# An order-only edge that places GpSimd's normalising product behind an addition of exponentials

## The chip, the cores and the metric

The kernel runs on one core of one Trainium2 chip. The metric is the device time of one execution in microseconds (us), as the median of several runs. For the kernel before it is 4073.38 us (three runs, 4070.07 to 4077.61).

## What is computed

Two layers on x of shape (2, 256, 64, 64), all in float32. The first is attention with 8 heads of depth 32 over n = 4096 positions, the second a non-local block with one softmax over 1024 pooled keys. Nearly all the time goes into the first, and the change lies in it:

```python
qkv = jnp.einsum('oc,bchw->bohw', w_qkv, x)
q, k, v = jnp.split(qkv, 3, axis=1)          # each reshaped to (b, 8, 32, 4096)
scores = jnp.einsum('bhdi,bhdj->bhij', q, k) / jnp.sqrt(jnp.asarray(d, x.dtype))
attn = jax.nn.softmax(scores, axis=-1)
out = jnp.einsum('bhij,bhdj->bhdi', attn, v)
return jnp.einsum('oc,bchw->bohw', w_proj, out.reshape(b, c, h, w)) + x
```

The softmax is normalised late: the kernel sums exp(scores - max) times v (the numerator, `num`) and exp(scores - max) alone (the denominator, `den`), and multiplies `num` by 1/`den` at the end of a block.

## The kernel before

**Tiling.** A block is one batch entry b, one group of four heads (`qd`, 0 or 1) and 512 queries (`i`, 0 to 7). There are 2 x 2 x 8 = 32 blocks, numbered 0 to 31 here in their order of time; n = 2b + qd is the index of the group of four heads, so blocks 0 to 7 have n = 0 and blocks 24 to 31 have n = 3. After blocks 15 and 31 come the output projection (`project`) and the second layer (`non_local`) of one batch entry.

**One block.** `attend` loops over j = 0 to 31, 128 keys at a time. In step j, for two pairs of heads, TensorE makes the scores into PSUM (line 401, with line 413 putting the maximum in first), and ScalarE takes the exponential (line 537): 128 x 1024 values for heads 0 and 1 into a tile of its own (`single`), and as many for heads 2 and 3 into one half of a double tile `two` (`double`), which serves j and j + 1. One step later TensorE multiplies by v (line 425, eight matmul pieces in the profile, into `w`), and VectorE adds `w` to `num` (line 436). Between these, TensorE, VectorE and ScalarE work on the maxima of a later block (lines 252, 264, 271, 278), cut into single steps by a generator. At some odd steps, q, k or v of a later block are made as well: in a block with i < 6, k and v of the next group at j = 15 and a q at j = 27. For n = 3 there is no next group, so these blocks have no k and v work at j = 15.

**The denominator** is summed on two roads. GpSimd adds the tile for heads 0 and 1 into the block's first such tile (line 455, called `added`). The double tiles of heads 2 and 3 are summed by DMAs that add while they write (line 463): GpSimd issues one for each pair of steps, into two running sums by turns. Each DMA holds its double tile until it has landed. There are `TWOS = 5` double tiles: two are the running sums, three go round, so the exponential of pair P writes to the tile that pair P - 3 has given back.

**Normalising** (`normalize`) of a block runs as a generator inside the next block: at j = 2 GpSimd issues a DMA that joins the two running sums (line 469); at j = 6 TensorE sums over partitions (`den`, line 481) and ScalarE copies the result to `r` (line 489); at j = 7 two DMAs on the SP queue spread the few distinct values over partitions (lines 498, 499); at j = 12 VectorE takes the reciprocals (line 503), and five DMAs on SP write them back and broadcast them into `r` (lines 504, 506); after 13 more steps, at j = 25, comes the product of line 511 on GpSimd, `y = num * r`. `advance(normal)` stands behind `add(blk, j, p, two)` in the loop, so at this point `added` is the addition of step j = 25 of the running block (of j = 24 in block 31, where VectorE takes the odd steps from GpSimd).

**Order.** The order in which instructions stand in an engine's queue isn't that of the source: a scheduler in the compiler chooses it by its own estimates of when operands are ready, and each engine then works through its queue in that order. `tc.issue_after(ins)` adds an edge without a semaphore: what is traced inside the block stands behind `ins` in the queue. The kernel has such edges already, for the joining DMA (line 468), the reciprocals (line 502) and the exponentials (line 536). In the built program of the kernel before, the product of line 511 stands directly behind the addition of step j = 13 in 29 of the blocks (j = 8 in block 31), and ahead of the DMA of line 463 for j = 12 and 13 (j = 8 and 9).

The pools that matter:

```python
    ONES, TWOS = 6, 5
    def single(name):
        return probs.tile([P, 2, NB], F32, tag="one", name=name, bufs=ONES)
    def double(name):
        return probs.tile([P, 2, 2, NB], F32, tag="two", name=name, bufs=TWOS)
```

Of the kernel before, what the change touches and what calls it, by code (L numbers as in the profile page):

```python
# [24 lines left out]
NB = 512  # L25
# [10 lines left out]
def conv_attention(  # L36
# [13 lines left out]
    nc = tc.nc  # L50
# [20 lines left out]
    def scratch(name):  # L71
        return ps_m.tile([P, NB], F32, tag="m", name=name)
# [303 lines left out]
    def attend(b, y):  # L376
# [65 lines left out]
        added = None  # L442
# [22 lines left out]
        def normalize(blk):  # L465
            whole = [1, 2]
            if (blk.qd, blk.i) != (QUADS - 1, NI - 1):
                with tc.issue_after(added.ins):
                    nc.gpsimd.dma_start(out=blk.sums[1], in_=blk.sums[2], accum_op=ALU.add)
                whole = [1]  # L470
                yield
            den = scratch(f"den_{blk.name}")
            mine = [
                [blk.sums[0], *blk.last],
                [blk.sums[n][:, j] for j in range(2) for n in whole],
            ]
            for n in range(max(map(len, mine))):
                for h in range(QH):
                    those = mine[h // 2]
                    if n < len(those):  # L480
                        nc.tensor.matmul(  # L481
                            den[bass.ts(h, D), :],
                            ones[:, :D],
                            those[n][:, h % 2, :],
                            start=(n == 0),
                            stop=(n == len(those) - 1),
                        )
            r = work.tile([P, NB], F32, tag="r", name=f"r_{blk.name}", bufs=1)
            nc.scalar.copy(r, den)
            yield  # L490
            if (blk.qd, blk.i) == (QUADS - 1, NI - 1):
                nc.vector.reciprocal(r, r)
            else:


                flat = [spare.tile([QH, NB], F32, tag=f"flat{a}", name=f"flat{a}_{blk.name}") for a in range(2)]
                few = work.tile([P, NB // D], F32, tag="few", name=f"few_{blk.name}")
                nc.sync.dma_start(out=flat[0], in_=r[::D, :])
                nc.sync.dma_start(out=few, in_=flat[0].rearrange("h (c e) -> (h c) e", c=D))
                for _ in range(5):  # L500
                    yield
                with tc.issue_after(reduced.ins):
                    nc.vector.reciprocal(few, few)
                nc.sync.dma_start(out=flat[1].rearrange("h (c e) -> (h c) e", c=D), in_=few)
                for h in range(QH):
                    nc.sync.dma_start(
                        out=r[bass.ts(h, D), :], in_=flat[1][h : h + 1, :].broadcast_to([D, NB])
                    )
                for _ in range(13):
                    yield  # L510
            nc.gpsimd.tensor_mul(y[:, blk.qd, bass.ts(blk.i, NB)], blk.num, r)

        waiting, normal = None, iter(())
        for qd in range(QUADS):
            for i in range(NI):
                blk = Block(qd, i)
# [3 lines left out]
                for j in range(NJ):  # L520
# [17 lines left out]
                    if waiting is not None:  # L538
                        weigh(*waiting)
                        if j == 0:  # L540
                            normal = normalize(waiting[0])
# [8 lines left out]
                    elif items and j in ((15, 27), (11, 19, 27))[len(groups) - 2]:  # L550
                        for item in items.pop(0):
                            advance(make(*item), 9)
        weigh(*waiting)
        return normalize(blk)


# [225 lines left out]
    for b in range(B):  # L782
        y = big.tile([P, NC, N], F32, tag="y", name=f"y{b}")
# [56 lines left out]
```

## Time and profile before

| what | value |
|---|---|
| median of 3 runs | 4073.38 us |
| the profiled execution: its time, its span in the trace | 4072.18 us, 4070.4 us |
| PE busy | 4021.6 us, 99% |
| DVE busy | 2974.8 us, 73% |
| ACT busy | 2673.8 us, 66% |
| POOL busy | 2892.5 us, 71% |
| granted TensorE clock, mean | 0.996 |
| line 511, the product: count, mean | 32, 1270 ns |
| POOL idle ahead of line 511 | 207.6 us |
| line 463, the adding DMA: count, median from issue to landing | 448, 7.6 us |

PE is TensorE, DVE VectorE, ACT ScalarE, POOL GpSimd, SP the engine that issues most plain DMAs. In the lists of waits, a row says who waited for whom, the total in us, how often, and the longest. In a timeline, a row has the start in us, the length in us, engine, line, operation, tiles and count; a bracket gives the idle time of the engine just before, and what ended it. A busy PE isn't a PE at its peak, since matmuls are pipelined and overlap in the records.

### The profile page before, as it was taken

What the parts mean: (1) busy time and instruction counts of PE and PEld (TensorE: products, weight loads), DVE (VectorE), ACT (ScalarE), POOL (GpSimd) and SP (SyncE); (2) the same over time, 40 slices, a digit from 0 to 9 for tenths busy, and PEclk for the clock granted to TensorE, in tenths of its full rate; (3) what the DMA queues carried; (4) which work ended last, traced back from release to release, by engine and by line L of the source; (5) the groups of instructions that cost most, each with busy time, mean ns of one, the idle gap of its engine ahead of it and who ended that gap; (6) DMA issues with size and microseconds to landing.
All of it is one profiled execution on the core that took longest, in us unless ns stands there. A gap on an engine that the chain in (4) does not pass through costs nothing.

```text
span 4070.4 us, 75211 instructions
## 1 busy us (share of the span) xinstructions
PE 4021.6 (99%) x29616; PEld 1495.2 (37%) x29616; DVE 2974.8 (73%) x5451; ACT 2673.8 (66%) x3329; POOL 2892.5 (71%) x1844
## 2 busy tenths in 40 slices
PE   9999999999999999999999999999999999999998
PEld 4333333333333333333333333333333333332333
DVE  5877877788778777774457777777888888784444
ACT  5777777777777777751147777777677777776111
POOL 0888887778778888761457888787888888776143
PEclk9999999999999999999999999999999999999999
DMA  1677777777777777780027777778777777778200
GB/s 59 143 161 161 155 164 160 159 162 164 156 161 163 165 161 160 165 197 0 25 51 159 161 161 162 165 160 173 161 165 161 158 155 164 154 151 173 76 16 26
DMA packets 113380, 569.35 MB, mean 140 GB/s; under 512 B 20232, under 2 KB 22024, under 8 KB 51840
## 3 DMA queue, kind: packets, MB, share of 16 engines
q0 software_dynamic: 68832, 501.25, 60.5%
q1 hardware_dynamic: 42928, 62.10, 5.0%
q8 instruction: 232, 3.80, 0.4%
q10 hardware_dynamic: 1264, 1.19, 0.1%
q14 instruction: 124, 1.02, 0.1%
HBM read 54.39 MB, written 8.88 MB: 16 GB/s over the span
## 4 chain that ended last, share of the span: by engine, by line
PE 89%; DMA 5%; DVE 2%; POOL 1%; issue 1%; ACT 1%; SPq 0%; POOLq 0%; DVEq 0%; ACTq 0%
PE ps L252 27%; PE w L425 23%; PE s L401 17%; PE y L698 5%; PE s L413 5%; DMA p<-p 3%; DMA flat<-few 2%; PE q L195 2%; PE den L481 1%; PE k L195 1%; PE proj L567 1%; PE g L623 1%; PE v L183 1%; DVE r L712 1%; PE f L666 1%
## 5 line engine op out<-in xcount | busy, mean ns | idle before, releaser
L455 POOL TENSOR_TENSOR p<-p,p 128x1024 f32<-128x1024 f32 x945 | 2331.0, 2467 | 444.5 <-ACT p L537 308.1
L252 PE MATMUL ps<-k,q 32*128 32x512 f32 x6232 | 2116.6, 618 | 2.4 <-DVE part L278 1.0
L537 ACT ACTIVATE p<-s 128x1024 f32<-128x1024 f32 x2048 | 1987.3, 1026 | 134.2 <-PE ps L252 46.1
L264 DVE TENSOR_REDUCE part<-ps 128x1 f32<-128x512 f32 x2136 | 1372.6, 686 | 138.2 <-PE s L401 66.4
L425 PE MATMUL w<-p,v 128*32 128x512 f32 x8192 | 1093.4, 605 | 0.0
L278 DVE CUSTOM_DVE_ANT_0 ps<-ps,over 128x512 f32<-128x512 f32 x980 | 683.8, 700 | 540.3 <-PE ps L252 299.1
L401 PE MATMUL s<-q,k 32*128 32x512 f32 x4096 | 1038.0, 594 | 0.0
L271 ACT ACTIVATE over<-ps 128x512 f32<-128x512 f32 x916 | 546.9, 597 | 578.2 <-PE ps L252 533.9
L252 PEld LDWEIGHTS ps<-k,q 32*128 32x128 f32 x6232 | 788.8, 184 | 261.6 <-DVE num L436 75.4
L436 DVE TENSOR_TENSOR num<-num,w 128x512 f32<-128x512 f32 x992 | 671.7, 677 | 42.3 <-PE w L425 39.4
L252 PE MATMUL ps<-kd,q 32*128 32x512 f32 x1056 | 568.4, 643 | 1.0 <-POOL kd L214 0.7
L401 PE MATMUL s<-q,last_kd 32*128 32x512 f32 x2048 | 515.2, 616 | 12.1 <-ACT p L537 12.1
L401 PE MATMUL s<-q,kd 32*128 32x512 f32 x2048 | 513.1, 617 | 2.0 <-ACT p L537 2.0
L252 PE MATMUL ps<-last_kd,q 32*128 32x512 f32 x904 | 482.1, 640 | 1.5 <-POOL last_kd L214 1.5
L425 PEld LDWEIGHTS w<-p,v 128*32 128x32 f32 x8192 | 161.5, 108 | 778.9 <-ACT over L271 689.4
L463 POOL DMA_DIRECT2D p<-p x448 | 388.4, 867 | 70.7 <-ACT p L537 67.4
L413 PE MATMUL s<-rows,ones_b 32*128 32x512 bf16 x2048 | 394.5, 381 | 0.1
L401 PEld LDWEIGHTS s<-q,k 32*128 32x128 f32 x4096 | 371.3, 184 | 10.6 <-issue 7.2
L413 PEld LDWEIGHTS <-ones_b 32*128 32x128 bf16 x2048 | 132.6, 91 | 504.4 <-PE ps L252 251.6
L401 PEld LDWEIGHTS s<-q,last_kd 32*128 32x128 f32 x2048 | 172.5, 184 | 232.4 <-ACT p L537 219.9
L401 PEld LDWEIGHTS s<-q,kd 32*128 32x128 f32 x2048 | 174.8, 185 | 224.4 <-ACT p L537 196.8
L698 PE MATMUL y<-p,kv 128*128 128x512 f32 x512 | 240.0, 608 | 6.4 <-DVE r L712 6.4
(106 smaller groups left out, 2239.7 us busy)
## 6 DMA issues: line engine op xcount, KB each, us to landing
p<-p POOLq DMA_DIRECT2D x478, 1024.0 KB, 7.6
x_k<-in_x_dram SPq DMA_DIRECT2D x32, 512.0 KB
x_q<-in_x_dram SPq DMA_DIRECT2D x30, 512.0 KB
x_res<-in_x_dram SPq DMA_DIRECT2D x16, 512.0 KB
out_dram<-z SPq DMA_DIRECT2D x16, 512.0 KB
r<-flat SPq DMA_DIRECT2D x120, 64.0 KB
x_v<-in_x_dram SPq DMA_DIRECT2D x6, 512.0 KB
wqk_sb<-in_wqk_dram ACTq DMA_DIRECT2D x1, 512.0 KB
```

What stands on the lines that cost most here:

```text
L252: nc.tensor.matmul(ps, q[n, i][bass.ts(h, D), bass.ts(g, P)], keys[bass.ts(h, D), :], start=True, stop=True,)
L264: reduced = nc.vector.tensor_reduce(part[:, g, h, j : j + 1], ps, AX.X, ALU.max)
L271: cut = nc.scalar.activation(over, ps, AF.Relu)
L278: reduced = nc.vector.tensor_tensor_reduce(out=ps, in0=ps, in1=over, scale=1.0, scalar=LEAST, op0=ALU.add, op1=ALU.max, accum_out=part[:, ...
L401: nc.tensor.matmul(s[:, t, :], kj[bass.ts(h, D), :], q[blk.n, blk.i][bass.ts(h, D), :], start=False, stop=True, skip_group_check=j % 2 == 1,)
L413: nc.tensor.matmul(s[:, t, :], ones_b[bass.ts(h, D), :], rows[blk.rows][bass.ts(h, D), :], start=True, stop=False,)
L425: nc.tensor.matmul(w[bass.ts(h, D), :], v[blk.n][:, keys(j), h, :], p[h // 2][:, h % 2, :], start=True, stop=True,)
L436: nc.vector.tensor_add(blk.num, blk.num, w)
L455: added = nc.gpsimd.tensor_add(blk.sums[0], blk.sums[0], p[0])
L463: nc.gpsimd.dma_start(out=blk.sums[n], in_=two, accum_op=ALU.add)
L537: nc.scalar.activation(p[pair], s, AF.Exp, scale=scale)
L698: nc.tensor.matmul(acc[i][o], wg[:, 2 * t + j, bass.ts(o, P)], p[:, j, :], **edge)
```

## The change

The product of line 511 is put inside an `issue_after` block, so that it can't stand ahead of the last addition of exponentials that was traced before it:

```diff
                 for _ in range(13):
                     yield
-            nc.gpsimd.tensor_mul(y[:, blk.qd, bass.ts(blk.i, NB)], blk.num, r)
+            with tc.issue_after(added.ins):
+                nc.gpsimd.tensor_mul(y[:, blk.qd, bass.ts(blk.i, NB)], blk.num, r)
```

In the built program 30 of the 32 products move. In 29 blocks the product goes from behind the addition of j = 13 to behind that of j = 25, and stands ahead of the DMA of line 463 for j = 24 and 25; in block 31 it goes from behind j = 8 to behind j = 24. The two products that belong to blocks 15 and 31 themselves, which are made in `project`, stay where they were. The queues of TensorE, VectorE, ScalarE and SP hold the same instructions in the same order as before, and the product waits for the same semaphores (four DMAs and VectorE).

## The prediction

> **What bounds the kernel now.** I read the page first: the busy times, then the chain that ended last.
>
> ```profile
> span 4070.4 us, 75211 instructions
> PE 4021.6 (99%) x29616; PEld 1495.2 (37%) x29616; DVE 2974.8 (73%) x5451; ACT 2673.8 (66%) x3329; POOL 2892.5 (71%) x1844
> PE 89%; DMA 5%; DVE 2%; POOL 1%; issue 1%; ACT 1%; SPq 0%; POOLq 0%; DVEq 0%; ACTq 0%
> ```
>
> TensorE is busy all the time, so an idle GpSimd costs nothing by itself. But 5% of the chain is DMA, which a kernel bound by TensorE alone wouldn't have. So I read the list of waits for the product and for what GpSimd feeds.
>
> ```profile
> POOL y L511 <- DMA r<-flat: 138.5, 25, 8.0
> POOL y L511 <- DVE r L492: 42.7, 2, 21.6
> POOL y L511 <- DVE part L264: 20.3, 4, 6.8
> ACT p L537 <- DMA p<-p: 25.9, 21, 3.2
> ```
>
> The product waits at the head of GpSimd's queue for the broadcast of reciprocals. Of 207.6 us, 42.7 belong to the two products in the projection, which stay; 164.9 us over 30 products are 5.5 us each. The last row matters: exponentials wait for adding DMAs. The timelines of block 29 (GpSimd, ScalarE, TensorE) show how one leads to the other.
>
> ```profile
> 3515.95 2.36 POOL L455 TENSOR_TENSOR p<-p,p 128x1024 f32<-128x1024 f32 x1 [0.57 <-ACT p L537]
> 3525.14 1.28 POOL L511 TENSOR_TENSOR y<-num,r 128x512 f32<-128x512 f32 x1 [6.83 <-DVE part L264]
> 3526.36 0.87 POOL L463 DMA_DIRECT2D p<-p  x1
> 3526.97 5.11 POOL L455 TENSOR_TENSOR p<-p,p 128x1024 f32<-128x1024 f32 x2
> ```
> ```profile
> 3534.29 1.02 ACT L537 ACTIVATE p<-s 128x1024 f32<-128x1024 f32 x1 [3.18 <-DMA p<-p]
> ```
> ```profile
> 3532.12 0.59 PE L252 MATMUL ps<-k,q 32*128 32x512 f32 x1
> ...
> 3535.37 0.70 PE L401 MATMUL s<-q,last_kd 32*128 32x512 f32 x2 [2.66 <-ACT p L537]
> ```
>
> The addition of j = 13 ends at 3518.31; the DMA behind the product is issued at 3526.36, 8.05 us late. Three pairs on, the exponential of j = 18 needs that double tile and waits 3.18 us, then TensorE stands 2.66 us. The chain of waits has the same order here (product, DMA 7.57 us, exponential, TensorE). The busy times of two stretches around it tell more:
>
> ```profile
> 3530.00:3536.00 6.00, 3.34 (x32) 0.78 (x24) 3.15 (x7) 2.82 (x5) 5.92 (x4) 1.00 0.92 190
> 3536.00:3540.00 4.00, 4.00 (x30) 1.64 (x26) 1.98 (x3) 1.66 (x3) 4.00 (x3) 0.62 0.86 178
> ```
>
> The third number from the right is the granted clock: 0.62 after the gap, and the score matmuls of that stretch take 1.06 us instead of 0.59. So a gap costs more than its length.
>
> **What the Trainium skill says.** "TensorE: Matmul & The Clock Gate", section "Architectural detail: the array is 16× 32×32, not 1× 128×128", says that GpSimd works strictly first in, first out; the trace agrees: nothing of GpSimd's runs in the 6.83 us. "DMA: Bandwidth & Descriptors", section "Anatomy of one DMA — SWDGE (gpsimd) path", says that a DMA's semaphore wait is done on the issuing sequencer, so a DMA of GpSimd's is held by what stands before it; the trace agrees (issued at 3526.36, 1.2 us behind the start of the product). The first page, section "What's actually happening", puts the fall to half clock after an idle window of about 3.4 us; here a gap of 2.66 us was followed by 0.62, so the measurement decides: less than 3.4 us can do.
>
> **The change, part by part.** It removes nothing and adds no semaphore; it moves 30 instructions on GpSimd's queue. The two products of the projection, SP's DMAs and the other engines' queues keep their places.
>
> *What leaves j = 13.* The adding DMA behind it, and all GpSimd work up to j = 25, comes earlier by the wait and the product itself: 5.5 + 1.27 = 6.8 us on average. What is it worth? In block 29 the DMA would have been issued at 3518.3 and landed at 3518.3 + 7.57 = 3525.9, and the exponential wanted the tile at 3534.29 - 3.18 = 3531.1: cover of 5.2 us without the product. Blocks with k and v work at j = 15 have more cover: their step there takes 6.83 us against 3.13 in n = 3, so 5.2 + 3.7 = 8.9 us. A mean delay of 6.8 us thus loses about 1.6 us in a block with n = 3 and nothing in most others, save where a landing is slow (10.33 us in block 4, by the chain). That is what the time line shows. I took the start of the v matmuls (line 425) of every step from TensorE's timeline; a block without loss takes 106.53 us, between 106.50 and 106.54 us in twelve blocks of n < 3, and its step 17 takes 2.99 us. The excess over the same step of undisturbed blocks, in steps 17 to 21 alone: block 4 1.48, 11 0.40, 14 0.39, 20 1.31, 23 0.82, together 4.4 us; blocks 24 to 30 (n = 3) 0.56, 2.02, 1.57, 0.88, 1.50, 4.49, 1.18, together 12.2 us. Block 31, where the product stands at j = 8 and waits 7.98 us: its steps behind the stall take 5.97, 4.14 and 3.20 us where their like take 2.37, 3.03 and 2.37, together 5.5 us. These sums hold the slow clock.
>
> *A second place.* In block 30 GpSimd never makes up its delay: 0.5 us per pair is all the slack it has (5.64 us of work in a pair of 6.1), seven pairs give 3.5 of the 7.3 us. Its last adding DMA is issued at 3682.38 instead of about 3679 (in block 25 the like one lies 4.1 us ahead of the next block's first v matmuls, which start at 3683.03 in block 31), then comes the joining DMA, and the sum over partitions waits for that. I put 3.0 us there, an estimate. Bounds: 0, if the DMAs land later anyway, to 4.0, the whole excess of that step (8.61 us against 4.64).
>
> *What comes to j = 25.* The product, 1.27 us, without a wait: its operands have been ready since j = 14. Queued behind it: the DMA of j = 24 and 25, two additions, the five small operations on the next maxima (lines 138 to 142), the last DMAs and the joining DMA. That DMA has a cover of 5.2 us, plus 2.8 us for the q work at j = 27 (5.79 against 2.99 us): 8.0 against 1.28. The maxima are read by TensorE 5.3 to 7.8 us after they are ready in most blocks; in block 30 only 0.6 us after, but there the delay of before (7.3 - 3.5 = 3.8 us) goes and 1.3 comes. At the end of block 2 GpSimd has idle stretches of 1.32, 0.90 and 1.95 us ahead of the last DMA, so 1.27 us is made up. I take 0 there. If that cover were gone, it would be 1.27 x 30 = 38 us. `num` has two buffers and `r` one: `num` is taken again at j = 1 and `r` at j = 6 of the next block, 8 and 13 steps later, so neither waits. `y` is read only in the projection.
>
> *Sum.* 4.4 + 12.2 + 5.5 + 3.0 = 25.1 us off the execution's own 4072.2 (span 4070.4 and 1.8 around it) gives 4047.1. That execution is 1.2 us under the median, so 4048.3 for the median. What limits next is TensorE itself: 12 blocks lose nothing today, and there is nothing to gain in those.
>
> **Rivals.** *Half of it stays.* Adding DMAs could be slow because their engines are full (share 0.92 and 0.86 in the windows above), and without pauses even more so; then some exponentials wait still. Against: with no delay a landing must take over 5.2 + 7.6 = 12.8 us to be waited for, and the longest of all is 12.6. With half of the 25 us: about 4061. *Nothing changes within what can be told.* Differences under 0.2%, 8 us, are about what a measurement of this kernel can't tell from none; this needs that the waits of ScalarE have another cause, such as the joining DMA (four of the 21 waits lie at j = 6 to 8, ahead of the stall) or SP's loads. Against: but for 0.14 us in block 10 and the place in block 31 above, all the losses lie in the steps behind the stall. About 4070. *Slower, by one mechanism:* GpSimd's end of block. If the product at j = 25 isn't made up, the last adding DMA, the joining DMA and the sum over partitions in the next block come 1.27 us late in each of 30 blocks, and TensorE waits: +38 - 25 = +13, so 4086. It decides from the point where GpSimd's idle time from j = 25 to the last DMA is under 1.27 us; block 2 has 4.2. That all 30 products move is settled by the built program; what remains is what it is worth.
>
> **How the numbers follow.** Chances: nearly full gain (4042 to 4057) 0.70, half 0.15 (up to 4065), nothing 0.09, slower 0.06. Up to 4065.2 (0.2% below 4073.4) counts as faster: 0.70 + 0.15 = 0.85; same 0.09; slower 0.06. The low end, 4042, is the sum with 4.0 instead of 3.0 for block 30, and with a median that lost 5 us more than the profiled execution did, as the slowest run of before (4077.6) suggests. The high end, 4064, takes in the case of half. Outside lie the 0.15 of the last two cases and a little of the half.
>
> **What would show it.** Right: GpSimd's wait for the broadcast of reciprocals falls from 138.5 us to about 0 (only the 42.7 for line 492 stays); ScalarE's wait for adding DMAs falls from 25.9 us to under 8; no gap of TensorE ahead of line 401; blocks 25 to 29 take about 102.8 us instead of 103.7 to 107.4. Wrong: waits of ScalarE for adding DMAs at j = 30 or in the next block's first steps, TensorE idle ahead of line 481 or 147 in many blocks, or blocks of n < 3 above 106.53 us.

## The result, and the profile after

The changed kernel takes 4047.81 us (median of six runs, 4044.66 to 4049.91) against 4072.64 us for the kernel before (six runs, 4067.81 to 4077.61): a ratio of 0.9938 with a 95% interval of 0.9925 to 0.9951, 24.8 us less. The forecast was 4048.3 us. The profiled execution took 4044.66 us.

The page of the changed kernel, the same three lines as before:

```profile
span 4042.9 us, 75211 instructions
PE 4010.2 (99%) x29616; PEld 1498.4 (37%) x29616; DVE 2968.7 (73%) x5451; ACT 2672.2 (66%) x3329; POOL 2893.4 (72%) x1844
PE 97%; DVE 2%; ACT 0%; POOL 0%; DMA 0%; issue 0%; DVEq 0%; ACTq 0%
```

No engine's work has changed by more than 12 us, but the DMA part of the chain that ended last is gone: 5% before, 0% now. The list of waits (who for whom, total us, times, longest; the product is now line 512, the exponential 538):

```profile
POOL y L512 <- DVE r L492: 42.8, 2, 21.6
ACT p L538 <- DMA p<-p: 0.7, 2, 0.4
PE s L401 <- ACT p L538: 0.2, 1, 0.2
```

Of the product's waits only the two in the projection are left. ScalarE waits for adding DMAs for 0.7 instead of 25.9 us. GpSimd's timeline in block 29, where the kernel before had its largest loss:

```profile
3504.16 2.36 POOL L455 TENSOR_TENSOR p<-p,p 128x1024 f32<-128x1024 f32 x1 [0.58 <-ACT p L538]
3506.45 0.87 POOL L463 DMA_DIRECT2D p<-p  x1
...
3541.01 2.36 POOL L455 TENSOR_TENSOR p<-p,p 128x1024 f32<-128x1024 f32 x1 [0.56 <-ACT p L538]
3543.33 1.29 POOL L512 TENSOR_TENSOR y<-num,r 128x512 f32<-128x512 f32 x1
3544.55 0.87 POOL L463 DMA_DIRECT2D p<-p  x1
```

The addition of j = 13 (the first row) is followed at once by its DMA, which was issued 8.05 us late before. Twelve steps later the product starts as soon as the addition of j = 25 is done, with no idle time ahead of it. The stretch of TensorE in which exponential j = 18 falls (busy times of the engines; the third number from the right is the granted clock):

```profile
3515.00:3521.00 6.00, 6.00 (x56) 2.16 (x52) 5.25 (x10) 4.73 (x7) 5.43 (x4) 1.00 0.90 184
3521.00:3525.00 4.00, 4.00 (x40) 1.30 (x37) 3.46 (x8) 3.49 (x5) 3.45 (x3) 1.00 0.96 199
```

TensorE is busy all through both windows, and the clock stays at 1.00 where it fell to 0.62.

**Where the 27.5 us between the two spans lie**, by the starts of the v matmuls (line 425) in both traces, each block counted from its first ones:

| stretch | before, start to start (us) | after (us) | gained (us) |
|---|---|---|---|
| up to block 0 | 103.20 | 102.67 | 0.5 |
| blocks 0 to 23 | 2852.56 | 2847.92 | 4.6 |
| blocks 24 to 30 | 727.27 | 714.71 | 12.6 |
| block 31, to its v matmuls of j = 30 | 92.34 | 82.54 | 9.8 |
| the rest | 295.03 | 295.03 | 0.0 |

Blocks 25 to 29 now take 102.82 or 102.83 us each (103.7 to 107.4 before), and the twelve blocks of n < 3 that the prediction took as undisturbed still take 106.5 us.

### The profile page after: what moved, and what is told of

It is laid out like the page before. It is cut to its first block, busy times and chain, and to the rows that moved or that the text cites. A ratio compares the mean times of both kernels' runs of the same rounds, so it can differ in the third digit from the quotient of the medians.

```text
span 4042.9 us, 75211 instructions
## 1 busy us (share of the span) xinstructions
PE 4010.2 (99%) x29616; PEld 1498.4 (37%) x29616; DVE 2968.7 (73%) x5451; ACT 2672.2 (66%) x3329; POOL 2893.4 (72%) x1844
## 4 chain that ended last, share of the span: by engine, by line
PE 97%; DVE 2%; ACT 0%; POOL 0%; DMA 0%; issue 0%; DVEq 0%; ACTq 0%
PE ps L252 30%; PE w L425 25%; PE s L401 19%; PE y L699 5%; PE s L413 5%; PE q L195 2%; PE k L195 2%; PE den L481 1%; PE v L183 1%; PE proj L568 1%; PE g L624 1%; DVE r L713 1%; PE f L667 1%; PE f L733 1%; PE tp L608 0%; PE tp L604 0%
```

## Experiments

**My theory:** the price is set by how late GpSimd issues the adding DMA that stands behind the product. A cover of 5.2 us (more in blocks with k and v work at j = 15) is free; what goes beyond it becomes a wait of ScalarE for a double tile, then a gap of TensorE, with slow clock after a long gap. **Rivals:** any GpSimd work at j = 13 costs in proportion; the waiting or the broadcast itself is what costs; the single tiles of heads 0 and 1 run out, not the double ones; or the new place costs something too, close to the end of the block.

### Delay without a wait: three, five and seven extra products at j = 13

```diff
+                    if before and j == (9 if last else 13):
+                        b4 = before[0]
+                        for _ in range(3):        # 5, 7
+                            with tc.issue_after(added.ins):
+                                stall = nc.gpsimd.tensor_mul(
+                                    y[:, b4.qd, bass.ts(b4.i, NB)], b4.num, b4.num)
+                        order.enter_context(tc.issue_after(stall.ins))
                     nc.gpsimd.dma_start(out=blk.sums[n], in_=two, accum_op=ALU.add)
```

`before[0]` is the preceding block, whose `num` is complete; `last` is true in block 31, where the hold stands at j = 9. The lines that fill `before` and open `order` are left out. The base is the changed kernel.

> The changed kernel, with three extra products (num times num, into columns of y that the true product overwrites later) on GpSimd between the addition of j = 13 and the adding DMA behind it, in each of the 30 blocks. Their operands are ready, so GpSimd is busy and waits for nothing. They hold the DMA back by 3 x 1.28 = 3.8 us. My theory (what counts is how late the adding DMA of the double tile is issued, and the cover is 5.2 us in n = 3 and more elsewhere): no loss, 4047 to 4050 us. Rival A (any GpSimd work at j = 13 costs in proportion; the kernel before lost 25 us to 6.8 us of delay): 14 us, about 4062. Rival B (the loss came from the semaphore wait or from the broadcast itself): no loss.

> The same with five extra products, 6.4 us, close to the mean delay of 6.8 us that the kernel before had from the wait and the product. My theory: the loss comes back, about 1.2 us and some slow clock in each block with n = 3, and some in block 31: 4063 to 4073 us, with ScalarE waiting for adding DMAs at j = 18. Rival A: 23 us, about 4071. Rival B (semaphore wait, or the broadcast's DMAs in the way of the adding DMAs): still no loss, 4048.

> The same with seven extra products, 9.0 us. My theory: beyond the cover the loss grows us for us: 9.0 - 5.2 = 3.8 us in the 7 blocks 24 to 30 and, since blocks with i = 6 or 7 have no k and v work at j = 15 either, in blocks 6, 7, 14, 15, 22 and 23, each with about 1.5 us of slow clock, 13 x 5.3 = 69 us, some 10 us in block 31, and up to 1 us in the 17 blocks whose cover of 8.9 us is just used up: 4125 to 4145. Rival A (in proportion): 33 us, about 4081. Rival B: 4048.

Measured: 4047.05 us with three (ratio to before 0.9933, 0.9916 to 0.9950), 4053.11 us with five (0.9948, 0.9934 to 0.9963), 4095.63 us with seven (1.0052, 1.0037 to 1.0067). GpSimd's timeline of the kernel with five, block 25, shows that I had mis-sized the hold:

```profile
3096.31 5.50 POOL L469 TENSOR_TENSOR y<-num 128x512 f32<-128x512 f32 x5
3101.92 0.87 POOL L473 DMA_DIRECT2D p<-p  x1
```

Five products in a row take 5.5 us, not 6.4, and seven 7.75. With these lengths the theory holds. 5.5 us is just over the cover of 5.2, and behind the hold only blocks 25 to 28 lose (1.6, 1.0, 0.2 and 0.9 us). What else is lost there lies at the end of block 30 (0.6) and in the step of block 31 with the sum over partitions (2.8), the second place of the prediction. With 7.75 us, ScalarE waits 2.3 us on average at j = 18 in blocks 24 to 30, against 7.75 - 5.2 = 2.55. The blocks lose 1.8 to 4.3 us, 2.7 on average: in blocks 27 and 29 slow clock comes on top (a granted clock of 0.57 and 0.61 in the 4 us behind their gaps). My forecast for seven products had counted slow clock in thirteen blocks as well. By the medians, growth isn't proportional: nothing at 3.3 us, 6 us in all at 5.5, 48 at 7.75, and 25 in the kernel before, whose delay is 6.8 us on average. So the first rival falls. The second falls too: nothing waits here for the broadcast, which is the same in all three runs and in the changed kernel, and the loss comes with the length of the hold.

One number didn't fit: the blocks with n < 3 and i < 6 lost 0.3 to 1.9 us each (15 us in all) at 7.75 us, inside the cover of 8.9 us that I had given them. The last experiment takes this up.

### The wait taken away, the place kept

```diff
-                for _ in range(5):
+                for _ in range(2):
                     yield
...
-                for _ in range(13):
+                for _ in range(16):
                     yield
-            nc.gpsimd.tensor_mul(y[:, blk.qd, bass.ts(blk.i, NB)], blk.num, r)
+            with tc.issue_after(adds.get(13, added).ins):    # the addition of j = 13
+                nc.gpsimd.tensor_mul(y[:, blk.qd, bass.ts(blk.i, NB)], blk.num, r)
```

> The kernel before, with the product kept directly behind the addition of j = 13 (j = 8 in block 31) by an edge, but with the reciprocals three steps earlier (2 empty steps instead of 5 ahead of them, 16 instead of 13 behind), so that the broadcast lands about 9 us sooner, ahead of the product. My theory (the wait costs, not the place): 4047 to 4051 us, GpSimd without a wait ahead of the product. Rival (the place costs: a product ahead of the adding DMA at j = 12 and 13 loses even without a wait): 4060 or more.

Measured: 4050.82 us (0.9942, 0.9927 to 0.9957). GpSimd's timeline in block 2 and then in block 31:

```profile
353.70 2.35 POOL L455 TENSOR_TENSOR p<-p,p 128x1024 f32<-128x1024 f32 x1 [0.53 <-ACT p L539]
356.02 1.27 POOL L513 TENSOR_TENSOR y<-num,r 128x512 f32<-128x512 f32 x1
357.24 0.86 POOL L464 DMA_DIRECT2D p<-p  x1
```
```profile
3696.93 1.26 POOL L513 TENSOR_TENSOR y<-num,r 128x512 f32<-128x512 f32 x1 [9.18 <-DMA r<-flat]
```

(`adds[j]` is kept by `add`: the addition of step j.) In blocks 1 to 30 the product stands where it stood before and doesn't wait, and these blocks take what they take in the changed kernel, within 0.3 us each. In block 31, where it still stands at j = 8, it waits 9.18 us and that block loses 5.1 us: a control inside the run, and more than the 3 us to the changed kernel. So a product that doesn't wait costs nothing at this place: its own 1.3 us are inside the cover.

### The adding DMA let past the product

```diff
-                    nc.gpsimd.dma_start(out=blk.sums[n], in_=two, accum_op=ALU.add)
+                    adds[j] = nc.gpsimd.dma_start(out=blk.sums[n], in_=two, accum_op=ALU.add)
...
-            nc.gpsimd.tensor_mul(y[:, blk.qd, bass.ts(blk.i, NB)], blk.num, r)
+            with tc.issue_after(adds.get(13, added).ins):    # the DMA of j = 12 and 13
+                nc.gpsimd.tensor_mul(y[:, blk.qd, bass.ts(blk.i, NB)], blk.num, r)
```

> The kernel before, with the product put directly behind the adding DMA for j = 12 and 13, so that this DMA is on time while the product still waits and holds what comes after it. My theory (late adding DMAs): the loss stays but moves by one pair, to the step of the exponential of j = 20 instead of j = 18, and is smaller, since GpSimd makes up 0.5 us in a pair: about 1.0 instead of 1.6 us in a block of n = 3: 4060 to 4068 us. Rival (late additions of heads 0 and 1, so that the single tiles run out): the loss stays in the same step, about 4072.

Measured: 4110.37 us (1.0092, 1.0077 to 1.0108), slower than the kernel before. The place of the loss is as I had said: step 17, where most of the loss had been, has none, and steps 19 and 21 have it (for instance 6.97 us in block 24, 6.46 in 27, 2.16 in 3). The size is not. The list of waits says why:

```profile
POOL y L512 <- DMA r<-flat: 213.7, 26, 9.4
ACT p L538 <- DMA p<-p: 57.4, 33, 6.3
```

In these 26 rows the product waits 8.2 us on average, instead of 5.5 before, though it stands one DMA issue (0.86 us) later. SP's timeline of block 25, first in the kernel before, then in this one:

```profile
3096.24 0.33 SPq L504 DMA_DIRECT2D flat<-few  x1
3102.86 1.72 SPq L506 DMA_DIRECT2D r<-flat  x4
```
```profile
3127.09 0.33 SPq L504 DMA_DIRECT2D flat<-few  x1
3133.81 3.83 SPq L506 DMA_DIRECT2D r<-flat  x4
```

From the first of these DMAs to the start of the product it is 10.1 us before (3106.37) and 13.5 here (3140.55); over the 30 blocks 9.1 to 11.6 before and 13.3 to 15.8 here. The last part of the broadcast now runs beside the adding DMA of 1 MB for j = 12 and 13. In the kernel before, the waiting product itself had held that DMA back. That the two share the DMA engines is the likely reason for the longer time; no run here changes only this. The rival with the single tiles, which has the loss stay in its step, falls.

### Fewer tiles of either kind

```diff
-    ONES, TWOS = 6, 5
+    ONES, TWOS = 5, 5     # the kernel before
+    ONES, TWOS = 6, 4     # the changed kernel
```

> The kernel before with 5 instead of 6 single tiles (heads 0 and 1), the double tiles as they were. My theory (the double tiles are what ScalarE waits for): single tiles have cover left, the time stays at 4070 to 4077 us. Rival (single tiles are what runs out): their cover falls by one step, 3.05 us, and the loss grows by this in every block that lost and in many that did not, 4100 us or more.

> The changed kernel with 4 instead of 5 double tiles: two go round instead of three. My theory: a double tile is taken for 3 x 6.12 - 5.2 = 13.2 us in its round; with two of them a pair can't take less than 6.6 us instead of 6.12, in 16 pairs of 32 blocks, less what the steps with q, k and v work give back: 4100 to 4270 us, with ScalarE waiting for adding DMAs in most pairs. Rival (double tiles aren't scarce): 4048 to 4055.

Measured: 4071.01 us with 5 single tiles (ratio 1.0000, 0.9992 to 1.0009), so a whole single tile was spare. 4452.08 us with 4 double tiles (1.0936, 1.0920 to 1.0953), with

```profile
ACT p L538 <- DMA p<-p: 411.4, 221, 7.7
```

in the list of waits. The double tiles are the scarce ones. The size was above my range, and the steps show what I had left out: most of the loss lies in steps 3 to 6 of a block (3.05, 1.37, 6.02 and 0.64 us in block 1), where the old block's running sums still hold tiles for the sum over partitions while the new block takes two of its own. That is a reading of the code beside the steps, not a test of its own. In other steps this block loses 4 us. More double tiles weren't tried; a sixth takes the space of two single tiles, of which only one was shown to be spare.

### How far the new place is from its limit

```diff
+                        if before and j == (21 if last else 25):
+                            b4 = before[0]
+                            for _ in range(5):
+                                with tc.issue_after(added.ins):
+                                    stall = nc.gpsimd.tensor_mul(
+                                        y[:, b4.qd, bass.ts(b4.i, NB)], b4.num, b4.num)
+                            order.enter_context(tc.issue_after(stall.ins))
```

> The changed kernel with five extra products (num times num, columns of y that are overwritten) behind the true product at j = 25 and ahead of the adding DMA for j = 24 and 25, so that GpSimd has 1.28 + 6.4 = 7.7 us there instead of 1.28. It asks how far the new place is from the point at which it would cost. My theory: the cover of that DMA is 8.0 us, GpSimd's idle time to the last DMA is 4.2 us, and the joining DMA has some 2.7 us more to the sum over partitions: 7.7 - 4.2 - 2.7 = 0.8 us in each of 30 blocks, some 4050 to 4075 us, with TensorE waiting ahead of line 481. Rival (the new place is close to its limit already): 6.4 x 30 = 192 us, about 4240.

Measured: 4062.91 us (0.9977, 0.9969 to 0.9986), 15 us above the changed kernel's own median. The five were meant to stand behind the true product; in the trace they stand ahead of the DMA and the true product directly behind it, so the DMA is held for 5.5 us and what follows for 6.8. Most blocks lose nothing; the losses lie in step 5 or 7 of ten blocks (2.65 us in block 31, 1.86 in 22, 1.76 in 6), behind the joining DMA, at the start of block 16 (1.6) and at the end of block 30 (4.2). GpSimd now waits ahead of the joining DMA (line 479 here):

```profile
POOL p L479 <- DMA p<-p: 28.1, 12, 3.4
```

So the slower rival of the prediction is real as a mechanism and has its place where it was put. The point from which it costs lies below 6.8 us of work at j = 25, how far below wasn't tried; the product's 1.3 us are still free.

### Other places for the product

```diff
-                for _ in range(13):
+                for _ in range(3):       # j = 15; range(17) for j = 29
                     yield
             with tc.issue_after(added.ins):
```

> The changed kernel with the product traced 10 steps earlier, so that its edge puts it behind the addition of j = 15, about when the broadcast lands. My theory (any place behind the landing does): 4046 to 4050 us. Rival (the distance to j = 25 matters, since the adding DMA of j = 14 and 15 is now in the same stretch as the broadcast): 4055 or more.

> The changed kernel with the product traced four steps later, behind the addition of j = 29, close to the end of the block. My theory (1.28 us fit wherever 5 us and more of cover are): 4046 to 4050 us. Rival (the end of the block has less cover, so the last adding DMA, the joining DMA and the sum over partitions come late): up to 1.3 x 30 = 38 us more, about 4085.

Measured: 4048.55 us at j = 15 (0.9941, 0.9926 to 0.9956), 4045.03 us at j = 29 (0.9932, 0.9917 to 0.9946). Neither interval parts them from the changed kernel's 0.9938. The run with j = 15 says more than I had asked. Its list of waits:

```profile
POOL y L512 <- DMA r<-flat: 80.5, 27, 4.0
```

The product waits 3.0 us on average, and no block from 1 to 30 loses over 0.12 us (block 31 2.0): 3.0 + 1.3 = 4.3 us is under the cover of 5.2. So a wait at the head of the queue was free here.

### The scheduler's own choice, with earlier data

```diff
-                for _ in range(5):
+                for _ in range(2):
                     yield
...
-                for _ in range(13):
+                for _ in range(16):
                     yield
             nc.gpsimd.tensor_mul(y[:, blk.qd, bass.ts(blk.i, NB)], blk.num, r)
```

The base is the kernel before.

> The kernel before with the reciprocals three steps earlier and no edge on the product: the scheduler then puts the product behind the addition of j = 10 instead of j = 13 (j = 8 in block 31), again ahead of its data. By the trace of the kernel with the edge, the broadcast lands about 3.7 us after that addition, so the product waits 3.7 us, and what stands behind it is 5.0 us late. My theory (a wait costs only what goes beyond the cover of 5.2 us): no loss in blocks 1 to 30 though the product waits in each, 4047 to 4053 us with block 31 losing about 5. Rival (the waits themselves cost, in proportion): 5.0/6.8 of the 25 us, about 4066.

Measured: 4063.66 us (0.9976, 0.9967 to 0.9984). The scheduler moved the product as far forward as the data had moved, and again it stands ahead of them. It waits 5.2 to 6.9 us in blocks 1 to 30, not 3.7. In the run with the edge nothing had waited for the broadcast, so the trace didn't show its landing; I had put it 2 us behind the issue of its last DMA, as in the kernel before, where the product kept the next adding DMA away from it. The lines of GpSimd's timeline for blocks 1 and 27:

```profile
247.00 1.27 POOL L512 TENSOR_TENSOR y<-num,r 128x512 f32<-128x512 f32 x1 [6.50 <-DMA r<-flat]
...
3299.89 1.28 POOL L512 TENSOR_TENSOR y<-num,r 128x512 f32<-128x512 f32 x1 [5.53 <-DMA r<-flat]
```

By time alone this run speaks for its rival (4066). By blocks it doesn't: blocks 1 to 23 lose nothing (0.2 us at most) though all that have a product wait, and blocks 24 to 30 lose 0.0 to 4.0 us, 10.1 us in all, with 27 the worst. The delay of 6.5 to 8.2 us (wait and product) is over 5.2 and under 8.9. Within blocks 24 to 30 the loss doesn't follow the delay alone: blocks 27 and 29 have the same delay (6.8 us) and lose 4.0 and 0.0. The trace shows why: the adding DMA that was held took 9.1 us to land in block 27 and 6.9 in block 29. So the theory stands, and my forecast failed on the length of the wait. Another 4.2 us of the time lie behind the v matmuls of block 31, with a gap of 2.3 us of TensorE in the projection; their cause stays open.

### Why blocks with n < 3 had less cover than I gave them

In the kernel with seven extra products, the chain of waits has these two adding DMAs (start, length) of blocks 2 and 25, and SP's timeline of block 2 a load of x beside the first:

```profile
364.50 9.62 DMA p<-p
```
```profile
3127.00 7.28 DMA p<-p
```
```profile
358.23 1.71 SPq L516 DMA_DIRECT2D r<-flat  x4
364.66 0.40 SPq L91 DMA_DIRECT2D x_q<-in_x_dram  x1
```

The load may start once TensorE has read the tile for the k and v work of j = 15, and this is when a late adding DMA of j = 12 and 13 is issued (in this kernel the two are 0.1 to 0.2 us apart in each of these blocks). The test leaves those loads out:

```diff
+        if attending and what == "q" and held:
+            held[b, i] = next(iter(held.values()))
         if (b, i) not in held:
```

> The kernel with seven extra products at j = 13 once more, without the loads of x for the q work of the attention blocks: q is made from the columns of x that lie in the tile already, so the outputs aren't the reference's. In blocks with n < 3 and i < 6 that load (512 KB on the SP queue) starts in the same microsecond as the adding DMA that the hold made late, and that DMA landed after 9.6 us in block 2, against 7.3 us in block 25. The question is why these blocks lost 0.3 to 1.9 us where a cover of 8.9 us against a delay of 7.75 us gave none. My theory (the load takes DMA time from the adding DMA): their loss, 15 us in all, falls to under 2 us, and the time from 4096 to about 4081 us, while blocks with i = 6 and with n = 3 keep theirs. Rival (the k and v work at j = 15 gives less cover than its length): no change in any block, 4094 to 4097.

Measured: 4079.51 us (1.0014, 1.0007 to 1.0020), against 4095.63 with the loads. Every block with n < 3 and i < 6 now loses 0.16 us or less (blocks 1 to 5: at most 0.03; with the loads 0.45 to 1.54). Blocks 6, 14 and 22 (i = 6, no k and v work at j = 15) keep 1.2 to 1.6, and blocks 24 to 30 keep 1.6 to 5.5. From issue to landing, the held adding DMA of the blocks with n < 3 and i < 6 took 9.0 to 11.0 us with the loads and 6.8 to 8.4 without.

The traces let the cover be worked out for the blocks that wait. Count from the end of the exponential of j = 13 to the landing of its DMA, and take off what ScalarE then waits at j = 18. In blocks 24 to 30 this gives 14.3 us in both the kernel before and the one with seven products (14.0 in block 29), for instance 9.22 + 8.04 - 2.96 in block 27 with seven products; in the waiting blocks with n < 3 and i < 6 it gives 18.0. Undisturbed, the DMA is issued 1.5 us after that end. With a landing of 7.6 us this leaves the 5.2 and 8.9 us of the prediction; with landings of 9.0 to 11.0 us the 8.9 shrink to 7.5 to 5.5. So the cover isn't one number: it is what the landing leaves of a fixed room.

## Why the prediction was right, point by point

- **What bounds it** held: TensorE, with short stops that start at GpSimd's product. The chain lost its DMA part, and the clock its dip.
- **Blocks with n < 3:** 4.4 us forecast, 4.6 measured (blocks 0 to 23).
- **Blocks 24 to 30:** 12.2 forecast, 12.6 measured. The cover of 5.2 us, read from a single block, is confirmed by the runs with a fixed delay: nothing at 3.3 us, first losses at 5.5, and waits of ScalarE of 2.3 us on average at 7.75.
- **Block 31 and the second place:** 5.5 + 3.0 = 8.5 forecast, 9.8 measured. The term that was too small is the 3.0 us for the late joining DMA: the step with the sum over partitions fell from 8.6 to 4.1 us, 4.5 us, even over the bound of 4.0, because I had taken the like step from blocks in which TensorE also works on maxima (4.64 us). Holds at j = 13 bring this loss back (2.8 us at 5.5, 4.5 at 7.75).
- **The start** (0.5 us up to block 0) isn't in the sum; the change touches nothing there. In the traces of the kernels with all their loads this stretch takes 102.7 to 103.7 us, so 0.5 us is within what executions differ by.
- **The product at j = 25 at no cost** held: no block of the changed kernel is longer than its undisturbed like. With 5.5 us of extra work there, a loss came.
- **A cover of 8.9 us in blocks with n < 3** was too much wherever the load of x starts with the DMA. This decided nothing in the sum, since their losses had been read off the timeline and not worked out from the cover. It does explain the slow landings: in blocks 4, 11 and 20 of the kernel before, where the product waited longest among the blocks with k and v work at j = 15, the load starts within 0.6 us of the adding DMA, which took 9.9 to 10.3 us to land. The prediction had laid all losses with n < 3 to slow landings. For blocks 14 and 23 that was wrong: their DMA landed after 6.8 us, and they have i = 6 and 7, so no k and v work at j = 15 and less cover.
- **Rivals.** *Half of it stays* and *nothing changes* fall: the waits of ScalarE for adding DMAs went from 25.9 to 0.7 us, though the DMA engines are as full as before (shares of 0.90 and 0.96 in the stretch shown). *Slower* showed itself only with the extra work.

The execution's own difference (27.5 us) is larger than that of the medians (24.8), as each is one draw of several runs that differ by 5 to 10 us. The parts in the trace come to 27.5 us against 25.1 forecast, so that the medians met the forecast within 0.5 us is partly luck.

That the slow clock follows from the length of the gap alone is not shown: in the kernel before, gaps of 2.66 us (block 29) and 1.84 us (block 31) were followed by 0.62 and 0.50, but one of 1.79 us (block 25) was followed by 1.00. With seven extra products even a gap of 2.18 us (block 28) was followed by 1.00. The two opposite cases, first from the kernel before and then from that with seven:

```profile
3728.20 2.08 PE L401 MATMUL s<-q,kd 32*128 32x512 f32 x4 [1.84 <-ACT p L537]
3728.20:3732.20 4.00, 4.00 (x16) 0.83 (x20) 2.83 (x1) 1.88 (x2) 2.63 (x2) 0.50 1.11 229
```
```profile
3452.99 0.70 PE L401 MATMUL s<-q,last_kd 32*128 32x512 f32 x2 [2.18 <-ACT p L548]
3453.00:3457.00 4.00, 4.00 (x36) 1.47 (x36) 2.51 (x5) 3.04 (x5) 3.97 (x3) 1.00 0.95 197
```

## What to carry to other kernels

An engine that is over a quarter idle can still set the time through what it issues. In this kernel an instruction that waited at the head of its queue held back the DMAs behind it, and the price was what the delay exceeded the cover of the buffers by: zero up to a point, then about us for us, with slow clock on top after some gaps. Find that cover in the trace before judging a wait: count from the natural issue of the DMA to the time when the buffer is wanted, and take the landing time with what else is on the DMA engines at that moment. Where a scheduler puts an instruction ahead of data that come by way of several DMAs, try an order-only edge to a later place. Here it cost nothing at the three places tried (j = 15, 25 and 29), but the place has a cover of its own: 6.8 us of work at j = 25 was too much.

## What the runs showed of the hardware that I hadn't expected

- A broadcast by four DMAs that write 64 KB each took longer, from 10.1 to 13.5 us in block 25 with the store ahead of it, where an adding DMA of 1 MB had been issued before its end.
- An adding DMA of 1 MB landed after 9.0 to 11.0 us when a load of 512 KB started with it, and after 6.8 to 8.4 us at the same place without the load.
- Products of 128 x 512 on GpSimd, 1.27 us when alone, took 1.10 to 1.11 us each in a row of five or seven.
- The clock fell after a gap of 1.84 us in one execution and not after one of 2.18 us in another, so in these runs the length of the gap alone doesn't tell.
